# Loading the masks of the scores ahead, and combining operands on VectorE, in a two-layer graph kernel

## Chip, cores and metric

One core of one Trainium2 chip. The metric is device time in microseconds (us); "median" is the median of a kernel's runs.

In the profile's lines PE is TensorE (PEld its weight loads), DVE VectorE, ACT ScalarE, POOL GpSimd and SPq SyncE, which issues loads; L104 is line 104 of the kernel before or after. The granted clock is TensorE's, as a share of full speed. An eviction is the copy or addition that takes a finished product out of the PSUM tile that the matmuls wrote.

## The reference, cut to what matters

The stage that the change touches computes, for `x` of 4096 x 512 and a symmetric sparse pattern `adj` of 4096 x 4096:

```python
h = x @ edge_w
e = h @ h.T                          # symmetric: half the tiles are computed, the rest transposed
e = jnp.where(adj > 0, e, NEG_BIG)   # every 512x512 tile of e needs its own 1 MB tile of adj
edge_att = jax.nn.softmax(e, axis=1)
...
output = adj * combined_att @ support
```

## The kernel before

Three stages: layer 0 (to 616 us), the scores `e` (616 to 1203 us), the aggregation `adj * att @ support` (from there to the end). In the scores stage a "couple" makes two neighbouring 512x512 tiles by seven half-size products instead of eight (`seven`), a "single" makes one tile. Tiles live in slots of 128x4x512 fp32. Each tile needs its own slot, its transposed tile needs another, and each of the two needs a mask slot.

```python
    free = deque(slots_p.tile([P, BG, W], F32, name=f"slot{n}") for n in range(13))

    def tick():                         # called after each half-product
        now[0] += 1
        if turns and turns[0][0] <= now[0]:
            turns.popleft()[1]()        # transposes of one row block (PE), copied out by ACT (L411)
        for _ in range(1 + (len(stats) > 6)):
            if stats:
                stats.popleft()()       # Rows.row, or a store
        for _ in range(1 + (len(exps) > 4)):
            if exps and exps[0][0] <= now[0]:
                exps.popleft()[1]()     # exponential (ACT, L368); the last one frees the mask's slot

    # in seven(): evictions of the products, each frees a PSUM bank
        def u2(ps, q, c11, c12, c21, c22):
            nc.vector.tensor_add(c12, c21, ps)                   # L104
        def u3(ps, q, c11, c12, c21, c22):
            nc.vector.tensor_add(c22, c21, ps)                   # L110
            nc.vector.tensor_add(c22, c22, banks[2][q])          # L111: c22 is complete
            after(q, 3)                                          # its transposes may follow
        # m4: L119, m3: L123 likewise on VectorE; m1, m2: copies on ScalarE (L101, L115)

    class Rows:
        def load(self):
            self.a = Uses(BG)           # takes a free slot
            nc.sync.dma_start(self.a.buf, adj[...])              # L354: the mask, 1 MB

        def row(self, i, s):
            b, c, a = self.r * BG + i, self.c, self.a.buf
            if self.fresh:              # L359: the mask's comparison
                nc.vector.tensor_scalar(a, a, 0.0, NEG_BIG, ALU.is_le, ALU.mult)
                self.fresh = False
            e = a[:, i, :]              # L362: a row of scores, with its minimum
            nc.vector.tensor_tensor_reduce(e, e, s.buf[:, i, :], -1.0, HUGE, ALU.add, ALU.min, accum_out=...)
            ...
    # ... cut: Pair, Single, the rest of Couple (the change's lines are in the diff below)

    for n, u in enumerate(units):
        ...
        events = deque((1 + 5 * double, r.load) for r in u.second)   # masks of the transposed tiles
        if nxt:
            events.append((2 + 5 * double, nxt.operands))
            if n:
                events += [(3 + 5 * double, r.load) for r in nxt.first]
```

The program's order is not the order of the built kernel: the builder arranges each engine's instructions itself.

Of the kernel before, what the change touches and what calls it, by code (L numbers as in the profile page):

```python
# [11 lines left out]
F32 = mybir.dt.float32  # L12
# [6 lines left out]
P = 128  # L19
# [7 lines left out]
def kernel(  # L27
# [13 lines left out]
    nc = tc.nc  # L41
# [13 lines left out]
    rows = ctx.enter_context(tc.tile_pool(name="rows", bufs=4))  # L55
# [22 lines left out]
    def seven(lop, rop, dests, after):  # L78




        K = len(rop(0))
        banks = [[ps_mm.tile([P, W], F32, name="seven", tag="mm") for q in range(2)] for _ in range(3)]

        def multiply(bank, m, first, then):
            for q in range(2):
                for k in range(K):
                    nc.tensor.matmul(  # L89
                        banks[bank][q],  # L90
                        lop(m, q)[k],
                        rop(m)[k],
                        start=(first and k == 0),
                        stop=(k == K - 1),
                        skip_group_check=not first,
                    )
                then(banks[bank][q], q, *dests[q])
                after(None, None)

        def m1(ps, q, c11, c12, c21, c22):  # L100
            nc.scalar.copy(c21, ps)  # L101

        def u2(ps, q, c11, c12, c21, c22):
            nc.vector.tensor_add(c12, c21, ps)  # L104

        def nothing(*_):
            pass

        def u3(ps, q, c11, c12, c21, c22):
            nc.vector.tensor_add(c22, c21, ps)  # L110
            nc.vector.tensor_add(c22, c22, banks[2][q])  # L111
            after(q, 3)

        def m2(ps, q, c11, c12, c21, c22):
            nc.scalar.copy(c11, ps)  # L115
            after(q, 0)

        def m4(ps, q, c11, c12, c21, c22):
            nc.vector.tensor_add(c21, c21, ps)  # L119
            after(q, 2)  # L120

        def m3(ps, q, c11, c12, c21, c22):
            nc.vector.tensor_add(c12, c12, ps)  # L123
            after(q, 1)

        multiply(0, 0, True, m1)
        multiply(1, 5, True, u2)
        multiply(2, 4, True, nothing)
        multiply(1, 6, False, u3)
        multiply(0, 1, False, m2)  # L130
        multiply(1, 3, False, m4)
        multiply(2, 2, False, m3)
# [14 lines left out]
    with (  # L147
# [111 lines left out]
        l11, l12 = we_s[:, :HK, :HD], we_s[:, HK:, :HD]  # L259
        l21, l22 = we_s[:, :HK, HD:], we_s[:, HK:, HD:]  # L260
        s4, s1, s2, s3 = (lops[:, n] for n in range(4))
# [5 lines left out]
        for g in range(HG):  # L267
            r11, r12 = (x1T[:, :HK, ts(c, W)] for c in (g, g + HG))
            r21, r22 = (x1T[:, HK:, ts(c, W)] for c in (g, g + HG))
            t1, t2 = (sp.tile([P, HK, W], F32, name="t12", tag="hi") for _ in range(2))  # L270
            t3, t4 = (sp.tile([P, HK, W], F32, name="t34", tag="lo") for _ in range(2))
# [41 lines left out]
    free = deque(slots_p.tile([P, BG, W], F32, name=f"slot{n}") for n in range(13))  # L313


    now = [0]
    turns, stats, exps = deque(), deque(), deque()

    def tick():
        now[0] += 1  # L320
        if turns and turns[0][0] <= now[0]:
            turns.popleft()[1]()
        for _ in range(1 + (len(stats) > 6)):
            if stats:
                stats.popleft()()
        for _ in range(1 + (len(exps) > 4)):
            if exps and exps[0][0] <= now[0]:
                exps.popleft()[1]()
# [46 lines left out]
    class Pair:  # L375
# [17 lines left out]
        def written(self, i):  # L393

            self.todo -= 1
            if not self.diag:
                stats.append(lambda: self.here.row(i, self.s))
                if not self.todo:
                    stats.append(lambda: self.store(self.A, self.B, self.s))
            turns.append((now[0] + 2, lambda: self.turn(i)))  # L400

        def turn(self, i):

# [16 lines left out]
    class Single:  # L420
# [5 lines left out]
        def operands(self):  # L426
            pass

        def main(self, between):
            (p,) = self.pairs  # L430
            p.begin()
            for i in range(BG):
                lo = i if p.diag else 0
                pe = ps_mm.tile([P, W], F32, name="pe", tag="mm")
                for k in range(KD):
                    nc.tensor.matmul(  # L436
                        pe[:, lo * P :],
                        hT[:, k, ts(p.A * BG + i, P)],
                        hT[:, k, (p.B * BG + lo) * P : (p.B + 1) * W],
                        start=(k == 0),  # L440
                        stop=(k == KD - 1),
                    )
                    if k % 2 and not (p.diag and i > 1):
                        between()
                nc.scalar.copy(p.s.buf[:, i, lo * P :], pe[:, lo * P :])
                p.written(i)

    class Couple:
# [8 lines left out]
        def operands(self):  # L457
            A, B, h = self.A, self.B, KD // 2
            if B not in Couple.right:
                r11, r12 = (hT[:, :h, ts(c, W)] for c in (B, B + 1))  # L460
                r21, r22 = (hT[:, h:, ts(c, W)] for c in (B, B + 1))
                t1, t2, t3, t4 = (lopp.tile([P, h, W], F32, name="right", tag="lop") for _ in range(4))
                nc.gpsimd.tensor_sub(t1, r12, r11)
                nc.gpsimd.tensor_sub(t2, r22, t1)
                nc.gpsimd.tensor_sub(t3, r22, r12)
                nc.gpsimd.tensor_sub(t4, r21, t2)
                Couple.right[B] = r11, r21, r22, t4, t1, t2, t3
            low, high = (hT[:, f : f + h, ts(A, W)].rearrange("p k (q u w) -> p k q u w", u=2, w=P) for f in (0, h))
            l11, l21 = (low[:, :, :, u, :] for u in range(2))
            l12, l22 = (high[:, :, :, u, :] for u in range(2))  # L470
            self.sums = Uses(1)
            s4, s1, s2, s3 = (self.sums.buf[:, n, :].rearrange("p (k q w) -> p k q w", k=h, w=P) for n in range(4))
            nc.gpsimd.tensor_add(s1, l21, l22)
            nc.gpsimd.tensor_sub(s2, s1, l11)
            nc.gpsimd.tensor_sub(s3, l11, l21)
            nc.gpsimd.tensor_sub(s4, l12, s2)
            self.left = l11, l12, s4, l22, s1, s2, s3

        def main(self, between):
            for p in self.pairs:  # L480
                p.begin()
            right = Couple.right[self.B]

            def follow(q, n):
                if q is None:
                    between()
                else:
                    self.pairs[n % 2].written(2 * q + n // 2)

            seven(  # L490
                lambda m, q: [self.left[m][:, k, q, :] for k in range(KD // 2)],
                lambda m: [right[m][:, k, :] for k in range(KD // 2)],
                [[p.s.buf[:, 2 * q + u, :] for u in range(2) for p in self.pairs] for q in range(2)],
                follow,
            )
            self.sums.used()

    panels = {}

    def panel(A):  # L500
# [174 lines left out]
    units = []  # L675
# [1 line left out]
        units += [Couple(A, B) for A in range(B)]  # L677
        units += [Single(B, B), Single(B, B + 1), Single(B + 1, B + 1)]
    blocks = [Aggregate(g, r) for g in range(HG) for r in range(HG)]
    for r in units[0].first + units[1].first:  # L680
        r.load()
    todo = deque()
    for n, u in enumerate(units):
        nxt = units[n + 1] if n + 1 < len(units) else None
        double = len(u.pairs) == 2
        events = deque((1 + 5 * double, r.load) for r in u.second)
        if nxt:
            events.append((2 + 5 * double, nxt.operands))
            if n:
                events += [(3 + 5 * double, r.load) for r in nxt.first]  # L690
        if n == len(units) - 3:
            todo.append(lambda: panel(0))
            todo.append(lambda: panel(HG))
            todo.extend(blocks[0].steps())
        passed = [0]

        def between():
            tick()
            passed[0] += 1
            while events and events[0][0] <= passed[0]:  # L700
                events.popleft()[1]()
            if todo:
                todo.popleft()()

        u.main(between)
        while events:
            events.popleft()[1]()
# [11 lines left out]
    for n, u in enumerate(blocks):  # L719
        nxt = blocks[n + 1] if n + 1 < len(blocks) else None  # L720
# [61 lines left out]
```

## Time and profile before

| before | |
|---|---|
| median, range | 2097.16 us, 2093.16 to 2098.34 (4 runs) |
| scores stage | 587.5 us; 465 us if all its units ran at the pace of the first ones |
| nine stalled couples / other couples | 38.3 us / 27.5 to 30.4 us each |
| PE's waits in the stage | 78.2 us: L104 47.1, L111 17.5, ACT L445 12.4, L411 1.2 |
| VectorE's waits at L359 for a mask | 146.0 us, 44 times |
| mean granted clock | 0.978, in the stage 0.93 |

The prediction below shows most of the lines. Two more are needed, from the page's list of costly groups (count, busy us, mean ns of one, idle time just before them and its main cause): the mask's comparison and the row of scores.

```profile
L362 DVE CUSTOM_DVE_ANT_0 slot<-slot,slot 128x512 f32<-128x512 f32 x256 | 181.3, 740 | 46.1 <-ACT slot L115 28.5
...
L359 DVE TENSOR_SCALAR slot<-slot 128x2048 f32<-128x2048 f32 x64 | 90.6, 1417 | 146.2 <-DMA slot<-in_adj_dram 146.0
```

The comparison is the place where VectorE stands still, and it does so for longer than it computes there.

### The profile page before, as it was taken

To read this page: it belongs to the slowest core of one execution; us is meant where nothing else is said; L and a number is where in the kernel's file an instruction comes from. 1 tells how busy PE (TensorE), PEld (TensorE's weight loads), DVE (VectorE), ACT (ScalarE), POOL (GpSimd) and SP (SyncE) were. 2 spreads that over 40 slices of the span, in tenths; PEclk is the share of its full clock that TensorE was granted. 3 is DMA by queue.
4 is the path that set the end of the run, shared out by engine and by line. 5 is a ranking of instruction groups with operands and counts; after the bars stand their busy time and mean duration, and the time that the engine had idled before them with its cause. 6 is when DMAs were issued, how large, how long until landed. Compare 5 with 4: busy or idle time off the path is not lost.

```text
span 2099.1 us, 17645 instructions
## 1 busy us (share of the span) xinstructions
PE 2003.9 (95%) x6170; PEld 1101.2 (52%) x6172; DVE 1340.2 (64%) x1879; ACT 663.1 (32%) x1147; POOL 507.4 (24%) x545
## 2 busy tenths in 40 slices
PE   9999999999999897898877999999999999999997
PEld 4888888887445443453433544444444444444443
DVE  3655555556446665656555888697669776877724
ACT  4333333333116464454544641122112311221100
POOL 0333333334132312131120111151113311240101
PEclk9999999999999998899998999999999999999999
DMA  8566556653026757475575897667667656765421
GB/s 323 187 217 207 197 204 216 207 199 118 20 86 236 269 209 267 174 283 198 204 275 212 318 404 283 229 237 275 229 217 261 258 199 223 269 236 215 174 86 60
DMA packets 118154, 455.73 MB, mean 217 GB/s; under 512 B 10289, under 2 KB 10289, under 8 KB 93489
## 3 DMA queue, kind: packets, MB, share of 16 engines
q0 software_dynamic: 48128, 241.20, 30.4%
q1 hardware_dynamic: 69360, 212.36, 29.7%
q8 instruction: 49, 0.80, 0.1%
q10 hardware_dynamic: 576, 1.05, 0.1%
q14 instruction: 41, 0.33, 0.0%
HBM read 355.99 MB, written 98.57 MB: 217 GB/s over the span
## 4 chain that ended last, share of the span: by engine, by line
PE 81%; DMA 11%; DVE 4%; ACT 3%; issue 1%; POOL 0%; POOLq 0%; DVEq 0%; SPq 0%
PE ps L604 37%; PE acc L209 11%; PE seven L89 11%; PE acc L208 11%; DMA slot<-in_adj_dram 10%; PE po L657 5%; PE pe L436 2%; ACT slot L368 2%; PE pt L410 2%; PE pw L181 1%; DVE slot L359 1%; DVE slot L362 1%; PE pt L238 1%; DMA s_d<-slot 1%; ACT slot L411 1%
## 5 line engine op out<-in xcount | busy, mean ns | idle before, releaser
L604 PE MATMUL ps<-slot,lop 128*128 128x512 f32 x1792 | 774.1, 592 | 0.0
L604 PEld LDWEIGHTS ps<-slot,lop 128*128 128x128 f32 x1792 | 339.9, 190 | 425.2 <-issue 414.2
L208 PE MATMUL acc<-xw,hi 128*128 128x512 f32 x1024 | 401.6, 392 | 0.0
L209 PE MATMUL acc<-xw,lo 128*128 128x512 f32 x1024 | 399.4, 390 | 0.5 <-DVE lo L205 0.5
L205 DVE TENSOR_TENSOR lo<-at,hi 128x1024 fp32r<-128x1024 f32 x128 | 169.0, 1320 | 146.8 <-ACT hi L203 146.8
L546 ACT ACTIVATE slot<-slot 128x2048 f32<-128x2048 f32 x64 | 122.0, 1911 | 394.1 <-DVE slot L543 394.1
L203 ACT CAST hi<-at 128x1024 fp32r<-128x1024 f32 x128 | 134.6, 1052 | 272.5 <-PE acc L208 271.2
L552 DVE SCALAR_TENSOR_TENSOR slot<-slot,slot 128x512 f32<-128x512 f32 x256 | 185.9, 779 | 51.2 <-DMA slot<-in_adj_t_dram 37.7
L368 ACT ACTIVATE slot<-slot,nmax_c 128x512 f32<-128x512 f32 x256 | 183.6, 720 | 108.2 <-DVE nmax_c L362 108.1
L209 PEld LDWEIGHTS acc<-xw,lo 128*128 128x128 f32 x1024 | 192.3, 188 | 41.0 <-DVE lo L205 1.7
L208 PEld LDWEIGHTS acc<-xw,hi 128*128 128x128 f32 x1024 | 192.3, 188 | 39.2
L362 DVE CUSTOM_DVE_ANT_0 slot<-slot,slot 128x512 f32<-128x512 f32 x256 | 181.3, 740 | 46.1 <-ACT slot L115 28.5
L543 DVE CUSTOM_DVE_ANT_1 slot<-slot,mrow 128x2048 f32<-128x2048 f32 x64 | 158.0, 2473 | 68.0 <-DMA slot<-s_d 66.8
L89 PE MATMUL seven<-right,slot 128*128 128x512 f32 x288 | 143.9, 652 | 47.1 <-DVE slot L104 47.1
L359 DVE TENSOR_SCALAR slot<-slot 128x2048 f32<-128x2048 f32 x64 | 90.6, 1417 | 146.2 <-DMA slot<-in_adj_dram 146.0
L608 DVE TENSOR_TENSOR over<-over,ps 128x512 f32<-128x512 f32 x168 | 113.3, 678 | 94.6 <-PE ps L604 94.6
L436 PE MATMUL pe<-hT 128*128 128x512 f32 (+3 forms) x384 | 135.0, 500 | 0.0
L538 POOL DMA_DIRECT2D slot<-in_adj_t_dram x64 | 49.2, 769 | 352.0 <-DVE slot L552 187.0
L89 PEld LDWEIGHTS seven<-right,slot 128*128 128x128 f32 x288 | 57.1, 204 | 122.8 <-issue 65.2
L410 PEld LDWEIGHTS pt<-ident,slot 128*128 128x128 f32 x496 | 63.7, 147 | 110.2 <-issue 75.7
L657 PE MATMUL po<-over 128*128 128x512 f32 x256 | 115.6, 599 | 3.6 <-DVE xb L666 3.6
L411 ACT COPY slot<-pt 128x512 f32<-128x512 f32 (+3 forms) x136 | 73.9, 546 | 131.4 <-PE pt L410 110.9
(124 smaller groups left out, 1884.0 us busy)
## 6 DMA issues: line engine op xcount, KB each, us to landing
at<-in_adj_t_dram SPq DMA_DIRECT2D x64, 1024.0 KB, 4.9
slot<-in_adj_dram SPq DMA_DIRECT2D x64, 1024.0 KB, 12.1
s_d<-slot POOLq DMA_DIRECT2D x64, 1024.0 KB, 7.8
slot<-s_d POOLq DMA_DIRECT2D x64, 1024.0 KB, 7.9
slot<-in_adj_t_dram POOLq DMA_DIRECT2D x64, 1024.0 KB, 7.3
lop<-lop_d SPq DMA_DIRECT2D x112, 512.0 KB, 3.8
xb<-in_x_dram SPq DMA_DIRECT2D x32, 256.0 KB, 3.0
x_d<-scr POOLq DMA_DIRECT2D x32, 256.0 KB, 2.5
```

The costliest lines, as they stand in the source:

```text
L89: nc.tensor.matmul(banks[bank][q], lop(m, q)[k], rop(m)[k], start=(first and k == 0), stop=(k == K - 1), skip_group_check=not first,)
L203: nc.scalar.copy(hi, aq)
L205: nc.vector.tensor_sub(lo, aq, hi.bitcast(F32))
L208: nc.tensor.matmul(acc, hi[:, c, :], xw[:, kb, :], start=(kb == 0), stop=False)
L209: nc.tensor.matmul(acc, lo[:, c, :], xw[:, kb, :], start=False, stop=(kb == NB - 1))
L362: nc.vector.tensor_tensor_reduce(e, e, s.buf[:, i, :], -1.0, HUGE, ALU.add, ALU.min, accum_out=nmax_c[:, b, c : c + 1])
L368: nc.scalar.activation(e, e, AF.Exp, bias=nmax_c[:, b, c : c + 1], scale=-1.0, accum_out=sum_c[:, b, c : c + 1])
L436: nc.tensor.matmul(pe[:, lo * P :], hT[:, k, ts(p.A * BG + i, P)], hT[:, k, (p.B * BG + lo) * P : (p.B + 1) * W], start=(k == 0), stop=(k ...
L543: nc.vector._custom_dve(TENSOR_ADD_SAT, out=q, in0=q, in1=mrow.unsqueeze(1).to_broadcast([P, BG, W]), s0=0.0, s1=-HUGE)
L552: nc.vector.scalar_tensor_tensor(qc, a[:, :, c, :], 0.0, qc, ALU.max, ALU.mult)
L604: nc.tensor.matmul(ps, lop[:, c, ts(h, P)], rop[m][:, c, :], start=(c == 0), stop=(c == BG - 1))
L657: nc.tensor.matmul(po, (lower if k // 2 else upper)[:, k % 2, ts(i, P)], w1_s[:, k, :], start=(k == 0), stop=(k == KD - 1),)
```

## The change

Intent: ask for every mask as soon as slots are free, in the order of need, so that no comparison waits for its load; and take the operand combinations off GpSimd, and out of a slot, so that GpSimd does not slow VectorE (one comparison took 2.50 us beside GpSimd's subtractions; the median of the 64 is 1.23) and a slot more is there for masks. Transposes come one tick later.

```diff
-            turns.append((now[0] + 2, lambda: self.turn(i)))
+            turns.append((now[0] + 3, lambda: self.turn(i)))
...
-                nc.gpsimd.tensor_sub(t1, r12, r11)        # and t2, t3, t4
+                nc.vector.tensor_sub(t1, r12, r11)        # and t2, t3, t4
...
-            self.sums = Uses(1)
-            s4, s1, s2, s3 = (self.sums.buf[:, n, :].rearrange(...) for n in range(4))
-            nc.gpsimd.tensor_add(s1, l21, l22)            # and s2, s3, s4
+            s2, s1, s3, s4 = (
+                rows.tile([P, h, 2, P], F32, name="left", tag="rows") for _ in range(4)
+            )
+            nc.vector.tensor_add(s1, l21, l22)            # and s2, s3, s4
...
-            self.sums.used()
...
-    for r in units[0].first + units[1].first:
-        r.load()
+    masks = deque(r for u in units for r in u.first + u.second)
+
+    def ahead(keep):
+        while masks and len(free) > keep:
+            masks.popleft().load()
+
+    ahead(4)
...
-        events = deque((1 + 5 * double, r.load) for r in u.second)
+        events = deque()
         if nxt:
-            events.append((2 + 5 * double, nxt.operands))
-            if n:
-                events += [(3 + 5 * double, r.load) for r in nxt.first]
+            events.append((9 if len(u.pairs) == 2 else 2, nxt.operands))
...
+            ahead(2 if any(p.t for p in u.pairs) else 4)   # after each half-product
```

More of the change, by code (lines that the diff above doesn't have):

```diff
@@ L462, in operands @@
                 t1, t2, t3, t4 = (lopp.tile([P, h, W], F32, name="right", tag="lop") for _ in range(4))
-                nc.gpsimd.tensor_sub(t1, r12, r11)
-                nc.gpsimd.tensor_sub(t2, r22, t1)
-                nc.gpsimd.tensor_sub(t3, r22, r12)
-                nc.gpsimd.tensor_sub(t4, r21, t2)
+                nc.vector.tensor_sub(t1, r12, r11)
+                nc.vector.tensor_sub(t2, r22, t1)
+                nc.vector.tensor_sub(t3, r22, r12)
+                nc.vector.tensor_sub(t4, r21, t2)
                 Couple.right[B] = r11, r21, r22, t4, t1, t2, t3
@@ L470, in operands @@
             l12, l22 = (high[:, :, :, u, :] for u in range(2))
-            self.sums = Uses(1)
-            s4, s1, s2, s3 = (self.sums.buf[:, n, :].rearrange("p (k q w) -> p k q w", k=h, w=P) for n in range(4))
-            nc.gpsimd.tensor_add(s1, l21, l22)
-            nc.gpsimd.tensor_sub(s2, s1, l11)
-            nc.gpsimd.tensor_sub(s3, l11, l21)
-            nc.gpsimd.tensor_sub(s4, l12, s2)
+            s2, s1, s3, s4 = (
+                rows.tile([P, h, 2, P], F32, name="left", tag="rows") for _ in range(4)
+            )
+            nc.vector.tensor_add(s1, l21, l22)
+            nc.vector.tensor_sub(s2, s1, l11)
+            nc.vector.tensor_sub(s3, l11, l21)
+            nc.vector.tensor_sub(s4, l12, s2)
             self.left = l11, l12, s4, l22, s1, s2, s3
@@ L684 @@
         nxt = units[n + 1] if n + 1 < len(units) else None
-        double = len(u.pairs) == 2
-        events = deque((1 + 5 * double, r.load) for r in u.second)
+        events = deque()
         if nxt:
-            events.append((2 + 5 * double, nxt.operands))
-            if n:
-                events += [(3 + 5 * double, r.load) for r in nxt.first]
+            events.append((9 if len(u.pairs) == 2 else 2, nxt.operands))
         if n == len(units) - 3:
```

## The prediction

> **What bounds the kernel now.** I read the page's 40 slices first, to find the stage where TensorE is not saturated.
>
> ```profile
> PE   9999999999999897898877999999999999999997
> PEclk9999999999999998899998999999999999999999
> DMA  8566556653026757475575897667667656765421
> ```
>
> A slice is 52.5 us. Only slices 12 to 22 dip, in PE and in clock: the stage that makes the scores from 616 to 1203 us. Before and after it PE is full, and the change leaves those stages' instructions alone. So the gain has to come from this stage. It consists of four groups of three single tiles (L436) and twelve couples (L89). I took unit boundaries from the PE timeline (a couple begins with its first two-operand `hT` matmuls) and asked for busy time per stretch.
>
> ```profile
> 616.00:649.80 33.80, 33.80 (x123) 19.35 (x122) 22.14 (x36) 16.64 (x41) 17.38 (x11) 1.00 0.92 342
> 755.25:895.97 140.72, 122.44 (x353) 58.41 (x352) 87.86 (x171) 69.14 (x169) 28.01 (x26) 0.92 0.57 212
> 936.20:1160.90 224.70, 185.39 (x530) 88.05 (x529) 133.59 (x292) 109.01 (x268) 33.08 (x40) 0.90 0.61 226
> 616.00:1203.55 587.55, 508.94 (x1562) 255.36 (x1561) 364.95 (x737) 303.04 (x740) 131.13 (x130) 0.93 0.65 242
> ```
>
> The columns are length, PE, PE load, DVE, ACT, POOL, clock, DMA share, GB/s. The first group of singles runs unstalled in 33.8 us, and the first couple (649.8 to 677.3) in 27.5 us. Twelve couples and four groups at that pace are 12 x 27.5 + 4 x 33.8 = 465 us. The stage took 587.5 us, so 122 us are lost. What PE waits for:
>
> ```profile
> PE seven L89 <- DVE slot L104: 47.1, 12, 7.7
> PE pt L410 <- DVE slot L111: 17.5, 9, 3.0
> ...
> 1060.81 3.67 PE L89 MATMUL seven<-right,slot 128*128 128x512 f32 x4 [3.45 <-DVE slot L104]
> ```
>
> All PE waits of the stage sum to 78.2 us. The other 44 us are work at a lower clock: the four matmuls after a stall take 3.67 us instead of 1.88. DVE is busy only 365 of 587 us, so it is late because it waits itself. Its wait list has one large entry, 146.0 us at the mask's comparison (L359) for the mask's load. The chain of one couple shows the loop:
>
> ```profile
> 1049.61 15.72 DMA slot<-in_adj_dram
> 1065.33 0.02 issue
> 1065.35 1.23 DVE slot L359
> ...
> 1067.21 0.70 DVE slot L111
> 1067.90 0.14 issue
> 1068.04 1.09 PE pt L410 x4
> ```
>
> An exponential frees a mask slot, the load takes 15.7 us, DVE stands at L359, and everything queued behind it is late (the evictions L104 and L111, then PE). Then the next couple does the same. Is it bandwidth? In 5 us windows of one couple:
>
> ```profile
> 1046.00:1051.00 5.00, 5.00 (x16) 2.48 (x15) 2.41 (x7) 4.05 (x11) 0.41 (x1) 1.00 1.02 372
> 1056.00:1061.00 5.00, 1.55 (x5) 0.48 (x4) 3.34 (x3) 0.00 (x0) 3.05 (x4) 1.00 1.05 399
> 1066.00:1071.00 5.00, 2.96 (x8) 1.81 (x9) 4.37 (x9) 1.43 (x4) 0.00 (x0) 0.68 0.00 0
> 1071.00:1076.00 5.00, 5.00 (x21) 2.85 (x20) 1.97 (x5) 4.32 (x11) 0.00 (x0) 0.98 0.00 0
> ```
>
> No: the DMA engines are full for about 20 us and then idle for over 10. Loads and stores of a couple are asked for in one burst at its boundary, because that is when slots come free and when the program asks. A load alone lands in 5.2 us, the median is 12.1 and the worst 18.6.
>
> [...] (3.67 against 1.88 us after a 3.45 us wait), so removing waits gives back more than their length. [...] one L359 took 2.50 us beside GpSimd's subtractions, 1.23 elsewhere. Taking those off GpSimd removes that. [...] the first five mask loads, issued within 2.3 us, land from 5.3 to 13.9 us after their issue. [...] the moved operations stay at about 0.68 us per 512 elements (L104: 678 ns).
>
> **The change part by part.**
>
> 1. Operand combinations from GpSimd to VectorE. GpSimd loses 48 left operations (16.9 + 15.7 + 16.6 + 16.5 us) and 12 right ones (29.3 us), 95 us in all. No PE wait names GpSimd, so directly this gives nothing. VectorE gains 48 x 0.68 = 33 us and 12 x 1.25 (128x1024, as L274 has it) = 15 us. Against that L359 should come down from 1.42 to about 1.23 us: 64 x 0.19 = 12 us. Per couple VectorE's work is 4 x 1.23 (masks) + 16 x 0.61 (L362, start to start) + 10 x 0.62 (evictions) = 20.9 us, and 4 x 0.68 more make 23.6 us. PE needs 27.5, so VectorE fits, at 86%.
>
> 2. The combinations live in four row buffers, so one of 13 slots is free for a mask. The buffers are single: the fourth combination must wait for the last product of the running couple. In the built order it stands just after that product's eviction, where VectorE loses little.
>
> 3. The masks. Before, four loads were asked for at fixed points around the couple's middle. Now each is asked for as soon as more than four (later two) slots are free, so nine are asked for at once at the start. The built order of the changed kernel shows what that leads to in a settled couple: its two first evictions (L104) have no L359 just ahead any more. That is the 47 us wait, and half of the clock loss. But three L359 stand together just ahead of L110. The loads that they need wait for slots freed by stores of the couple before. Estimate, from the boundary of the couple (T): the first store starts at about T-4 and lands by T+1, the slots of the first two loads are free at T+1 to T+2, and they land by T+9. The third load waits for the store of a transposed tile. Its last transpose comes after T+2, its store goes at T+4 and lands near T+12, and the load lands near T+18, at 2.7 us for each transfer in the queue. PE makes the sum that L110 evicts ready by T+14. So VectorE still stands for some 4 to 6 us, then has about 12 us of work left. PE tolerates about 4 us of that, the two half-products between. I get a couple of about 30 to 31 us rather than 27.5.
>
> 4. Turns one tick later: the transposes wait less for L111, of the 17.5 us most should go, at the price of a later store.
>
> Sum. The nine stalled couples took 344.7 us in all, 38.3 each; at 30.8 they take 277: 67 us won. The first couples of the three groups are unchanged (27.5, 27.5, 30.4). The three stalled groups of singles (40.9, 40.2, 42.7) lose 22 us against 33.8; the same burst causes it, and I count half, 11 us. Together 78 us: 2098 - 78 = 2020 us.
>
> **Rivals.**
>
> A. Everything hides: the look-ahead spreads the burst and PE is bound throughout. 8 MB per couple at 2.7 us for each MB are 21.6 us, less than 27.5, and VectorE's 23.6 fit too. Then nearly all 122 us go, about 1985 us. Against it: VectorE takes its queue in order, and L359 ahead of L110 waits for slots that free late.
>
> B. The wait only moves, from L104 to L110 and L111, because a load cannot start before its slot is free: 13 slots hold eight tiles per couple for some 40 us each. For it: three L359 before L110, and loads behind stores. Then couples stay at 34 to 36 us, and the time at about 2060 us.
>
> C. VectorE becomes the bound: 48 us more on it, with waits on its own chain, and a wait on a row buffer blocks everything behind it. At a busy share of 86% that makes 32 to 33 us per couple, 2040 us. The trace before shows 11 us of waits for masks in a couple, which are to vanish, so there is room.
>
> D. Loads hidden anyway: excluded, since the chain runs through them.
>
> **Range and chances.** The couple's length decides: 1 us of it is 9 us of time. 28 us gives about 1993, 34 gives 2049. I set 1985 to 2052. Two per cent faster means below 2055.9, a win of 42 us, which fails only if B holds nearly in full: faster 0.88, same 0.11. Slower needs a new stall of 80 us in this stage with nothing won, 0.01.
>
> **What would show it.** L104 must vanish from PE's waits (47.1 us to under 10). VectorE's 146 us at L359 should fall to 50 to 80, now ended by loads whose slots came from stores. The stage's clock should rise from 0.93 to above 0.97, L359 fall to near 1.25 us, the DMA's idle windows inside a couple shrink. The stage should end near 1125 us instead of 1203, with the aggregation after it of equal length. I am wrong if PE's waits keep their sum under L110, L111 or a row buffer (B, C), if the couple is under 28.5 us (A), or if the later stage changes length.

## The result, and the profile after

| | before | after |
|---|---|---|
| median, range (4 runs each) | 2097.16 (2093.16 to 2098.34) | 2069.27 (2067.24 to 2073.12) |
| scores stage | 587.5 us | 561.2 us |
| mean granted clock; in the stage | 0.978; 0.93 | 0.981; 0.94 |
| PE's waits in the stage | 78.2 us | 68.5 us |
| VectorE's waits at L359 for a mask | 146.0 us | 108.0 us |
| POOL busy, DVE busy (whole kernel) | 507.4, 1340.2 us | 412.8, 1357.3 us |

The ratio is 0.9872, 95% interval 0.9852 to 0.9893. Ratios here are the mean time of one kernel's fast runs over that of the other's of the same rounds, so not quite the ratio of the medians quoted. All outputs are right. The kernel is 1.3% faster; 2020 us was predicted, in 1985 to 2052. About a third of the predicted gain came: **the prediction was wrong**.

The page's 40 slices of the kernel after still dip over the same slices:

```profile
PE   9999999999999998798878899999999999999997
...
PEclk9999999999999999899989999999999999999999
```

The dip is a little shallower than before, not gone. Busy time per stretch in the kernel after (columns as in the prediction: length, PE, PE load, DVE, ACT, POOL, clock, DMA share, GB/s): the whole stage, then two 5 us windows of one couple.

```profile
614.30:1175.50 561.20, 492.35 (x1563) 253.92 (x1562) 375.52 (x792) 305.69 (x739) 39.46 (x71) 0.94 0.68 257
...
997.10:1002.10 5.00, 1.48 (x4) 0.38 (x2) 1.82 (x2) 0.59 (x1) 0.00 (x0) 1.00 1.04 397
...
1007.10:1012.10 5.00, 5.00 (x12) 2.27 (x11) 3.72 (x10) 3.73 (x10) 0.00 (x0) 0.69 0.00 0
```

Full DMA engines and an almost idle PE, then a working PE at a low clock and no transfer at all: the burst at the couple's boundary is still there. After the stage, the kernel before took 2099.1 - 1203.55 = 895.6 us and this one 2071.4 - 1175.5 = 895.9 us, so everything that was won was won in the stage. PE's waits in the stage, kernel after (us in all, times, longest):

```profile
PE pt L410 <- DVE slot L111: 56.0, 9, 9.6
PE pt L410 <- ACT slot L445: 6.6, 1, 6.6
PE seven L89 <- DVE slot L104: 4.6, 2, 4.4
```

L104 went from 47.1 to 4.6 us, as predicted. L111 went from 17.5 to 56.0: the wait moved from the second product's eviction to the third's. One couple shows how. It begins at T = 982.08 us. The chain of waits of the kernel after (start, length, what):

```profile
988.99 13.79 DMA slot<-in_adj_dram
1002.77 0.02 issue
1002.80 1.23 DVE slot L359
...
1004.66 0.70 DVE slot L111
1005.36 0.14 issue
1005.49 1.09 PE pt L410 x4
```

From the load on it is the same loop as before the change, link for link; only this load's slot was freed by a store (landed at 988.94 us) and not by an exponential. VectorE's timeline of the same kernel and couple (start, length, in brackets the idle time before it and what ended that):

```profile
995.64 1.23 DVE L359 TENSOR_SCALAR slot<-slot 128x2048 f32<-128x2048 f32 x1 [3.33 <-DMA slot<-in_adj_dram]
1000.09 1.23 DVE L359 TENSOR_SCALAR slot<-slot 128x2048 f32<-128x2048 f32 x1 [3.23 <-DMA slot<-in_adj_dram]
...
1002.80 1.23 DVE L359 TENSOR_SCALAR slot<-slot 128x2048 f32<-128x2048 f32 x1 [0.89 <-DMA slot<-in_adj_dram]
1003.94 0.68 DVE L110 TENSOR_TENSOR slot<-slot,seven 128x512 f32<-128x512 f32 x1
```

And PE's:

```profile
996.70 1.88 PE L89 MATMUL seven<-hT 128*128 128x512 f32 x4
1005.49 1.09 PE L410 MATMUL pt<-ident,slot 128*128 128x128 f32 x4 [6.91 <-DVE slot L111]
1006.37 3.62 PE L89 MATMUL seven<-hT 128*128 128x512 f32 x4
```

Three comparisons stand ahead of L110, and each waits for its load, 7.45 us together. The product that L110 evicts was ready long before: by 996.70 us PE is in the next one. It ends that half-product at 998.6 us, stands 6.91 us, and runs the next four matmuls in 3.62 us rather than 1.88. No row of scores starts on VectorE between 991.00 and 1007.06 us. So the three masks were used by nothing until after the very evictions that their comparisons held up.

That the wait for a mask is a matter of *where the comparison stands in the queue*, and not of how early the load is asked for, was at this point only a reading of the trace. The experiments test it.

### The profile page after: what moved, and what is told of

The parts are those of the page before. It is cut to its first block, busy times and chain, and to the rows that moved or that the text cites. A ratio compares the mean times of both kernels' runs of the same rounds, so it can differ in the third digit from the quotient of the medians.

```text
span 2071.4 us, 17608 instructions
## 1 busy us (share of the span) xinstructions
PE 1986.4 (96%) x6172; PEld 1099.3 (53%) x6172; DVE 1357.3 (66%) x1939; ACT 666.1 (32%) x1147; POOL 412.8 (20%) x485
## 4 chain that ended last, share of the span: by engine, by line
PE 79%; issue 8%; DMA 8%; DVE 4%; ACT 1%; POOL 0%; POOLq 0%; DVEq 0%; SPq 0%
PE ps L603 37%; PE acc L209 11%; PE acc L208 11%; PE seven L89 9%; PE po L656 5%; DMA slot<-in_adj_dram 5%; DMA s_d<-slot 2%; PE pe L436 1%; PE pt L410 1%; PE pw L181 1%; DVE slot L362 1%; PE pt L238 1%; ACT slot L368 1%; DVE slot L359 1%; DMA slot<-s_d 0%
## 5 line engine op out<-in xcount | busy, mean ns | idle before, releaser
L362 DVE CUSTOM_DVE_ANT_0 slot<-slot,slot 128x512 f32<-128x512 f32 x256 | 168.2, 688 | 44.0 <-ACT slot L411 20.9
L359 DVE TENSOR_SCALAR slot<-slot 128x2048 f32<-128x2048 f32 x64 | 78.2, 1225 | 108.0 <-DMA slot<-in_adj_dram 108.0
L410 PE MATMUL pt<-ident,slot 128*128 128x128 f32 x496 | 83.0, 290 | 64.2 <-DVE slot L111 56.0
L390 POOL DMA_DIRECT2D s_d<-slot x64 | 34.8, 545 | 530.1 <-ACT slot L411 354.0
L410 PEld LDWEIGHTS pt<-ident,slot 128*128 128x128 f32 x496 | 65.8, 150 | 139.7 <-issue 115.9
L89 PE MATMUL seven<-right,left 128*128 128x512 f32 x288 | 128.6, 599 | 4.6 <-DVE slot L104 4.6
L436 PE MATMUL pe<-hT 128*128 128x512 f32 (+3 forms) x384 | 130.1, 486 | 0.0
```

What stands on the lines that cost most here:

```text
L89: nc.tensor.matmul(banks[bank][q], lop(m, q)[k], rop(m)[k], start=(first and k == 0), stop=(k == K - 1), skip_group_check=not first,)
L410: nc.tensor.transpose(pt[:, j, :], self.s.buf[:, i, ts(j, P)], ident)
L436: nc.tensor.matmul(pe[:, lo * P :], hT[:, k, ts(p.A * BG + i, P)], hT[:, k, (p.B * BG + lo) * P : (p.B + 1) * W], start=(k == 0), stop=(k ...
```

## The experiments

Theories, as the expectations name them:

- **Q, the queue.** The comparisons stand too early in VectorE's queue. Put behind the evictions, the same loads are early enough.
- **S, the slots.** A load cannot start before a slot is free. With 13 slots the loads are late wherever the comparison stands.
- **V, VectorE.** The moved combinations make VectorE the bound.
- **P and F,** for the second part of the change: what it is worth comes from GpSimd no longer slowing the VectorE instructions that run beside it (2.50 us at one comparison, 1.23 at the median; P), or from the slot it no longer takes (F).

Each median is beside the kernel before on the same chip (2095.04 to 2096.4 us there).

### Comparisons behind the evictions, everything else as after

This edit, the **tie**, orders each comparison behind the last couple eviction that the program wrote before it. It synchronises nothing and adds no instruction (VectorE has 1939 in both kernels); it forbids the builder to put the comparison ahead of that eviction. The builder then arranged more of VectorE's queue anew, rows of scores and combinations too; the sequence of SyncE's loads stayed as it was. It shifts the line numbers: in the tied kernels L104 is L107, L110 and L111 are L113 and L114, L359 is L362, L362 is L367, L410 is L415, L445 is L450.

```diff
+ORDER = mybir.DependencyInfo(mybir.DependencyClass.NoSync, mybir.DependencyReason.DATA)
...
+    evicted = [None]
...
-            nc.vector.tensor_add(c12, c21, ps)       # L104; L111, L119, L123 likewise
+            evicted[0] = nc.vector.tensor_add(c12, c21, ps)
...
-                nc.vector.tensor_scalar(a, a, 0.0, NEG_BIG, ALU.is_le, ALU.mult)
+                cmp = nc.vector.tensor_scalar(a, a, 0.0, NEG_BIG, ALU.is_le, ALU.mult)
+                if evicted[0] is not None:
+                    tc.add_manual_dep(cmp.ins, evicted[0].ins.name, ORDER, reason="masks after evictions")
```

> The changed kernel, with each mask comparison tied, in VectorE's order only, behind the last couple eviction that the program wrote before it; no load, slot or operation differs. Theory Q (queue order: TensorE stands because comparisons of masks that are needed half a couple later were placed ahead of the evictions, and VectorE takes its queue in order): TensorE's wait for L111, 56.0 us after the change, falls under 15, couples go from 36.6 to 29 to 31 us, time 2005 to 2030 us. Theory S (slots: the masks come too late for their own use, since slots come free late): the wait moves to the masks' own use, couples stay at 35 us or more, time 2055 to 2075. Theory V (VectorE is the bound with its new work): couples 33 to 34 us, time about 2040, VectorE busy over 90% inside a couple.

Measured: 1987.15 us (1986.14 to 1987.72), ratio 0.9475 (0.9461 to 0.9489), 82 us below the changed kernel's 2069. Clock 0.997. Couples take 27.3 to 27.8 us. That is better than Q's 2005 to 2030 us and 29 to 31 us. The stage as one stretch, up to the last transposes as in the kernel after, then all that is left of PE's waits in it, then VectorE's timeline at the first eviction of one couple:

```profile
614.50:1090.60 476.10, 471.08 (x1567) 245.15 (x1566) 364.18 (x781) 302.01 (x737) 43.20 (x71) 1.00 0.81 300
```

```profile
PE pt L415 <- ACT slot L450: 5.0, 2, 3.6
```

```profile
915.38 0.69 DVE L107 TENSOR_TENSOR slot<-slot,seven 128x512 f32<-128x512 f32 x1 [1.55 <-PE seven L92]
915.98 1.22 DVE L362 TENSOR_SCALAR slot<-slot 128x2048 f32<-128x2048 f32 x1
```

The comparison follows the eviction and finds its mask there; this mask had landed 48 us before. PE is busy 471.08 of 476.10 us at full clock, VectorE 364 us, and its waits for masks fell from 108.0 to 4.6 us. What follows the stage took 1985.7 - 1090.6 = 895.1 us, as before.

The loads did not become earlier. The couple shown for the kernel after (T = 982.08 us) begins at 936.62 us in this kernel. Its four mask loads are asked for 3.8 to 11.2 us after its start and land 15.3 to 24.1 us after it; without the tie it was 1.3 to 12.2 and 13.5 to 23.4. But the comparisons of these four masks now start 23 to 38 us after the landing, where without the tie three of the four started at the landing itself. So Q holds, though the tie did not separate the comparisons' place from the rest of the new order. V falls: the same VectorE work fits with nearly a quarter of the stage to spare. So does S as the main cause: the same slots suffice.

### The tie alone, on the kernel before

> The kernel before with the same tie and nothing else of the change. Theory Q: here too the L104 wait (47.1 us) comes from a comparison that stands ahead of it, so the tie alone takes 40 to 80 us off 2097, though loads asked for late leave part of the wait. Theory S: within 10 us of 2097, the loads being late for their use.

Measured: 2045.41 us (2040.53 to 2047.88), ratio 0.975 (0.9731 to 0.977). The tie by itself does more than the whole change does by itself, within Q's 40 to 80 us. PE's largest wait left in this kernel:

```profile
PE pt L415 <- DVE slot L114: 28.2, 8, 5.0
```

VectorE waits only 5.6 us for masks here, so this remainder is not a mask's wait. What it is, the next experiments ask.

### Each part of the change alone, without and with the tie

Masks ahead (and the third tick) alone: the changed kernel with the combinations back on GpSimd and in a slot.

```diff
-                nc.vector.tensor_sub(t1, r12, r11)        # and the seven others
+                nc.gpsimd.tensor_sub(t1, r12, r11)
...
-            s2, s1, s3, s4 = (rows.tile([P, h, 2, P], F32, name="left", tag="rows") for _ in range(4))
+            self.sums = Uses(1)
+            s4, s1, s2, s3 = (self.sums.buf[:, n, :].rearrange(...) for n in range(4))
...
+            self.sums.used()
```

> Masks ahead and turns one tick later, but the combinations on GpSimd in a slot as before. Theory Q: the placement of the comparisons decides, so about the changed kernel's 2069, within 12 us. Theory S: one slot less for masks makes it clearly worse than 2069, 2080 or more. Theory V: better than 2069, since VectorE is relieved.

Measured: 2080.5 us (2078.52 to 2081.05), ratio 0.9921 (0.9904 to 0.9938). That lies at the edge of Q's range and of S's alike, so it decides nothing between them; V's forecast fails.

Operands alone: the kernel before with the operands' part of the change, the reverse of the edit above, and nothing else.

> Combinations on VectorE in the row buffers, masks asked for as before. Theory Q: within 10 us of 2097, for the comparisons still stand ahead of L104. Theory S: a small gain from the freed slot, 10 to 20 us. Theory V: slower than before, 2105 or more.

Measured: 2095.53 us (2090.97 to 2096.76), ratio 0.9988 (0.997 to 1.0006): nothing. But PE's waits in it are other ones than before the change; this is the largest:

```profile
PE pt L410 <- DVE slot L111: 73.2, 12, 11.6
```

L104's wait is all but gone in this kernel too (1.5 us), and L111's took its place. The time is in Q's range, but not for Q's stated reason, comparisons ahead of L104. So the look-ahead was not needed to drive the stall from L104 to L111: the operands' part and the built order that came with it did that, with the masks asked for at the old points.

Then both with the tie. Masks ahead, combinations on GpSimd, tie:

```diff
 # the masks-alone kernel
+# the tie, as in the first experiment
```

> The tie in VectorE's order together with the masks asked for ahead, combinations left on GpSimd in a slot. With the tie alone the kernel took 2045, with the whole change and the tie 1987. If the early loads are what the tie lets work (theory Q), this is near 1987: 1985 to 2005, with VectorE's wait for masks under 15 us. If the combinations on VectorE or their slot matter, 2020 or more.

Measured: 2018.38 us (2017.54 to 2023.03), ratio 0.9638 (0.9618 to 0.9659). VectorE's waits for masks are 8.8 us, as Q said; the time missed Q's range and nearly reached the other, so the combinations matter.

The kernel before, operands on VectorE in row buffers, tie:

```diff
 # the operands-alone kernel
+# the tie, as in the first experiment
```

> The tie with the combinations on VectorE, masks asked for as before. Theory Q: near the tie alone, 2035 to 2050, since masks asked for late are late. If the combinations' place is the larger part of the 58 us, 2010 or less.

Measured: 1988.25 us (1986.69 to 1990.02), ratio 0.9493 (0.9472 to 0.9514). This was a surprise, and Q's 2035 to 2050 us failed: it lacks the masks' look-ahead and is as fast as the whole change with the tie. The eight kernels, as ratios to the kernel before:

| combinations / masks | GpSimd, slot / fixed | VectorE, rows / fixed | GpSimd, slot / ahead | VectorE, rows / ahead |
|---|---|---|---|---|
| builder's order | 1 | 0.9988 | 0.9921 | 0.9872 |
| tie | 0.9750 | 0.9493 | 0.9638 | 0.9475 |

Without the tie the operands' part is worth nothing alone; with it, 57 us (2045 to 1988). The likely reason, argued and not measured, is that with the comparisons in the way VectorE lost at the next comparison what the other part saved. The look-ahead, with the third tick that comes with it, is worth 27 us with the tie while the combinations are on GpSimd, and 1 us, within the noise, once they are not. How much of the 27 us is the tick's was not measured; PE's largest wait was at L114 there (28.2 us), which a tick may shorten.

### The third tick

```diff
-            turns.append((now[0] + 3, lambda: self.turn(i)))
+            turns.append((now[0] + 2, lambda: self.turn(i)))
```

On the changed kernel:

> The changed kernel with the transposes two ticks after the eviction again instead of three, no tie. TensorE stands at the transposes for L111, so one tick less (2.15 us of products) lets it stand up to 2.15 us longer in each of nine stalled couples; but the transposed tiles' stores go 2.15 us earlier, and with them the load on which VectorE stands. Theory Q: the two nearly cancel, 2069 within 10 us. If only the first counts, 2080 to 2090.

Measured: 2078.76 us (2077.03 to 2079.71), ratio 0.9921 (0.9902 to 0.994): 9.5 us slower, just inside Q's range.

On the changed kernel with the tie:

> The changed kernel with the tie and the transposes after two ticks. TensorE stood for 5 us in all with three ticks, so VectorE has its evictions done in time: within 8 us of 1987. If the third tick was needed for the evictions, TensorE waits for L111 again and it takes 2000 or more.

Measured: 1985.83 us (1985.32 to 1986.86), ratio 0.9479 (0.9462 to 0.9496), against 0.9475 with three ticks: the same. The third tick gives PE one more half-product before it meets a late L111. That is worth about 10 us where L111 is late, and nothing where it is not.

### A fourteenth slot

The clean test of S: more slots, comparisons left in the builder's order. The room came from two of the four buffers of a small tile.

```diff
-    free = deque(slots_p.tile([P, BG, W], F32, name=f"slot{n}") for n in range(13))
+    free = deque(slots_p.tile([P, BG, W], F32, name=f"slot{n}") for n in range(14))
...
-        mrow = pan.tile([P, W], F32, name="mrow")
+        mrow = pan.tile([P, W], F32, name="mrow", bufs=2)
```

> The changed kernel without the tie, with 14 slots instead of 13 (room made by two fewer buffers for a row of maxima that is used later). Its built order has the same three comparisons ahead of L110. Theory Q: a slot more makes the loads a little earlier, but the comparisons are then placed earlier too: 2050 to 2070, far from 1987. Theory S (slots are what is short): most of the 82 us between 2069 and 1987 goes, 2010 or less.

Measured: 2069.15 us (2067.13 to 2072.21), ratio 0.9879 (0.9843 to 0.9915); the changed kernel has 0.9872. PE's largest wait in the stage, and VectorE's for masks, in this kernel:

```profile
PE pt L410 <- DVE slot L111: 48.1, 8, 9.0
```

```profile
DVE slot L359 <- DMA slot<-in_adj_dram: 104.3, 39, 8.3
```

108.0 us of waits for masks became 104.3. One slot more is not what was missing; more than one was not tried.

### What the operands' part is worth: the engine or the slot

With the tie, four kernels differ only in the engine of the eight combinations and in the place of the left ones. Two are above; these are the other two. Row buffers, but on GpSimd (from the 1988 us kernel):

```diff
-                nc.vector.tensor_sub(t1, r12, r11)        # and the seven others; the row buffers stay
+                nc.gpsimd.tensor_sub(t1, r12, r11)
```

> The tie, masks as before, combinations in the row buffers but on GpSimd. Tie alone: 2045; tie with the combinations on VectorE in row buffers: 1988. Theory P ([...] L362's successor had a mean of 858 ns with the tie alone and 685 without GpSimd's work, 44 us over 256): as slow as the tie alone, 2030 to 2060, that mean at 800 ns or more. Theory F (the freed slot or the buffers): 1985 to 2000.

Measured: 2017.39 us (2013.24 to 2018.51), ratio 0.9624 (0.9594 to 0.9654).

In a slot, but on VectorE (from the 2045 us kernel):

```diff
-                nc.gpsimd.tensor_sub(t1, r12, r11)        # and the seven others; the slot stays
+                nc.vector.tensor_sub(t1, r12, r11)
```

> The other half: the tie, masks as before, combinations on VectorE but in a slot taken from the 13 as before. Theory P: the engine matters and not the place, 1985 to 2000, mean of the score row's instruction under 700 ns. Theory F: 2030 or more.

Measured: 2011.29 us (2006.8 to 2014.12), ratio 0.9596 (0.9565 to 0.9628).

| with the tie | GpSimd | VectorE |
|---|---|---|
| left combinations in a slot | 2045 | 2011 |
| left combinations in row buffers | 2017 | 1988 |

Neither time fell into a range of P or of F. Each theory is half right: the engine is worth 34 or 29 us, the place 28 or 23, and the two nearly add up. The engine's share shows in the row of scores. In the groups of the stage (count, busy us, mean ns), the four kernels in the order slot and GpSimd, rows and GpSimd, slot and VectorE, rows and VectorE:

```profile
L367 DVE CUSTOM_DVE_ANT_0 slot<-slot,slot 128x512 f32<-128x512 f32 x256 | 208.7, 858 | 31.4 <-ACT slot L450 16.6 <-issue 7.5 <-ACT slot L416 4.8
```

```profile
L367 DVE CUSTOM_DVE_ANT_0 slot<-slot,slot 128x512 f32<-128x512 f32 x256 | 193.5, 798 | 34.7 <-ACT slot L450 18.8 <-ACT slot L416 13.3
```

```profile
L367 DVE CUSTOM_DVE_ANT_0 slot<-slot,slot 128x512 f32<-128x512 f32 x256 | 164.6, 686 | 27.1 <-ACT slot L450 12.7 <-ACT slot L416 12.4
```

```profile
L367 DVE CUSTOM_DVE_ANT_0 slot<-slot,slot 128x512 f32<-128x512 f32 x256 | 165.1, 685 | 34.7 <-ACT slot L450 20.5 <-ACT slot L416 12.2
```

GpSimd makes the mean row 113 to 172 ns longer. The timelines of the kernel with row buffers and GpSimd show single cases, VectorE first, then GpSimd:

```profile
847.76 2.82 DVE L367 CUSTOM_DVE_ANT_0 slot<-slot,slot 128x512 f32<-128x512 f32 x1
...
859.45 0.69 DVE L367 CUSTOM_DVE_ANT_0 slot<-slot,slot 128x512 f32<-128x512 f32 x1
```

```profile
847.24 2.80 POOL L469 TENSOR_TENSOR right<-hT,right 128x1024 f32<-128x1024 f32 x1
```

The same VectorE instruction takes 2.82 us beside a GpSimd one and 0.69 us alone. In the kernel before with the tie this costs, by an estimate from the means, 256 x (858 - 685) ns = 44 us at the rows and 64 x (1410 - 1239) ns = 11 us at the comparisons. That is 55 us of VectorE's time, more than it takes VectorE to make the combinations itself: 48 x 0.68 + 12 x 1.22 = 47 us, with the durations of the tied change's trace.

The slot's share is less clear. In the kernel with the slot on VectorE a combination waits 2.76 us for the store that frees its slot, and PE waits 17.1 us for L114. But the built order differs as well, and no run here separates the two.

## Why the prediction was wrong, point by point

**What bounds the kernel: right.** The stage, its loop and the 465 us it would take unstalled held: with the tie the stage is 476.1 us, 5.0 of them waits of PE, and its couples take 27.3 to 27.8 us. The stages after it kept their length (895.6 and 895.9 us).

**The operands' part as a cost: right.** GpSimd's busy time fell by 94.6 us (95 expected), the comparison's mean from 1417 to 1225 ns (1.23 us expected). VectorE's busy time in the stage rose by only 10.6 us (365.0 to 375.5), in part because the rows of scores got shorter too, 740 to 688 ns (13 us), which the prediction left out. That "directly this gives nothing" held for the kernel as built (0.9988) and hid the 57 us that it gives with the tie.

**The masks' part: here it failed.** The prediction saw the mechanism: "three L359 stand together just ahead of L110", behind loads whose slots come from stores. It mis-sized what follows: when the loads land, how long PE can bridge, and so the couple's length. Its estimates for the couple, T being the couple's boundary, and what the couple at T = 982.08 us showed:

| estimate | predicted | measured |
|---|---|---|
| the first load lands | by T+9 | T+13.5 (issued at 983.37, landed at 995.61) |
| the second | by T+9 | T+18.0 (landed at 1000.07) |
| the third's slot is free | near T+12 | T+6.9 (its store landed at 988.94) |
| the third lands | near T+18 | T+20.7 (its load alone took 13.79 us) |
| PE tolerates | about 4 us | one half-product; it ended at 998.6 us and PE stood 6.91 us |
| low clock after the stall | not in the couple's sum | 3.62 us for four matmuls rather than 1.88 |
| couple | 30 to 31 us | 36.6 us, mean of nine |

The couple adds up: 27.5 us unstalled, 6.91 us of standing and some 2.4 us of slower work after it (two half-products with their transposes in 6.66 us, from 1005.49 to 1012.15, where later ones took 2.15 each) make 36.8; it took 36.97. The slot came sooner than estimated and the load still landed later: when the third load was asked for, at 988.99 us, two of GpSimd's stores were under way (to 994.19 and 998.25 us), the DMA share was 1.04 in the window from 997.1 us shown above, and the load took 13.79 us. The shortest mask load of the kernel before took 5.2 us, with two others beside it for part of that time; this is the prediction's "load alone". The loads were counted at 2.7 us each one behind the other (the first five of the kernel before landed 2.71 us apart, from 621.66 to 632.50 us), with none of the couple's other traffic beside them. These five, which land 5.3 to 13.9 us after their issue, are loads of one queue, and did not show what loads and stores do to each other.

**The third tick: right in direction, in the wrong place.** It was said to take most of the 17.5 us at L111 away. That wait grew to 56.0 us, though without the tick the kernel would have been about 10 us slower.

**The sum.** The nine stalled couples fell from 344.7 to 329.6 us, so 15 us were won there where 67 were predicted: this term is the error. The three first couples won 2 us (0 predicted). The singles won 157.6 - 148.1 = 9.5 us (11 predicted); these 148.1 include 8.8 us as the aggregation begins, 6.64 of them a wait. In all 26 us, which is the stage's 587.5 - 561.2.

**The rivals.** B, "the wait only moves, from L104 to L110 and L111", is what happened: it gave 2060 us, the runs 2069. Two of the prediction's own signs said so: PE's waits kept 68.5 of 78.2 us, now under L111, and VectorE's waits for masks fell to 108.0 us, not to 50 to 80. B's mechanism was named rightly; its ground, too few slots, was not, since a fourteenth slot gave nothing and with the tie 13 suffice. C fell: VectorE had room. A, everything hides at about 1985 us, is what the tie brought (1987.15). The prediction named the obstacle to A, "VectorE takes its queue in order" (in the couple shown L110 started at 1003.94 us, behind three comparisons that waited 7.45 us, and by 996.70 PE was past its product), and took the order as given. It gave B too small a chance, although the three comparisons ahead of L110 were in the built order for all to see.

**Where the expected gain went.** It went into a new wait. The loop was never "a load is asked for too late", but "a comparison stands ahead of evictions, and its load is not there yet". Asking earlier did not cure that: in the kernel after, 41 comparisons still waited for their load. That the builder places a comparison as if its load were there fits this, but no run shows its rules.

## What to carry to other kernels

VectorE took its queue in order, so a comparison that waited for a transfer delayed everything behind it (L110 by 7.45 us in the couple shown). Look at what stands *behind* the waiting instruction, and whether that is what the bound engine needs. Before a load is moved earlier, try to move its first user later, behind what is urgent; here 82 us lay in that, with no load and no buffer changed in the program, while the change itself won 28. And a part that measures as nothing alone may be hidden by another stall: repeat it once the stall is gone (0.9988 became a step from 0.9750 to 0.9493).
